# SyncE instead of GpSimd as the issuer of the transfers in a branch that is not taken: a graph-attention layer with layer norm

## The chip, the core and the metric

The kernel runs on one core of a Trainium2 chip. The time is device microseconds from launch to end, the median of several runs. A profile is one execution with a record of every instruction and every transfer; its span reaches from the first to the last instruction.

The engines are TensorE (PE; its weight loads are PEld), VectorE (DVE), ScalarE (ACT), GpSimd (POOL) and SyncE (SP), which computes nothing and here issues transfers. Each has an instruction queue of its own, run in order (in the views PEq or PEldq, DVEq, ACTq, POOLq, SPq are the parts that handle branches, semaphores and issues), and each waits for the others through counts (semaphores).

## The reference

One graph-attention layer with four heads, added to its input, then a layer norm of each row:

```python
# x (4096, 512), adj (4096, 4096), W (512, 4*512), a (4, 2*512, 1), all float32
ht = (x @ W).reshape(N, 4, 512).transpose(1, 0, 2)
src = einsum('hnd,hd->hn', ht, a[:, :512, 0])
dst = einsum('hnd,hd->hn', ht, a[:, 512:, 0])
e = leaky_relu(src[:, :, None] + dst[:, None, :], 0.01) + adj[None]
att = softmax(e, axis=-1)
out = layernorm(x + einsum('hij,hjd->hid', att, ht).mean(axis=0), axis=-1)
```

The non-zero entries of adj lie between 0.05 and 1e9, so in most rows the softmax is decided by the largest entry of adj alone. Then the row's attention is a one-hot vector, and the sum over nodes is a gather of one row of x.

## The kernel before

The kernel has two paths. `gat_resnorm_kernel` (L27) runs the usual path, `leading_rows` (L67), then reads a flag and runs `general` (L529) if the flag is over zero:

```python
    flag = nc.values_load(any_bad[0:1, 0:1], min_val=0, max_val=N)
    with tc.If(flag > 0, preferred_fallthrough_block=True, label="general"):
        general(tc, x, adj, W, out, ident, v, n_bad)
```

**The usual path** takes the 4096 rows in 32 blocks of 128 (partition p of block ib is row 32p + ib). A loop over t (L409) has its stages written out by hand: adj blocks are loaded five ahead on SyncE (L118), VectorE finds each row's largest entry by segments of 32 (L163 and L170 to L172), GpSimd gathers the segment (L176) and then the row of x that the largest entry names (L186) with indirect transfers, TensorE turns the gathered row (L213) and multiplies it by the mean of the four heads' W (L228), ScalarE and GpSimd make the statistics of the layer norm (L250 to L257) and ScalarE writes the result (L261). SyncE stores the finished rows at the end, in this order (L465 to L468 for the first ones, and then):

```python
    for ib, n in ((NB - 4, 1), (NB - 3, 1), (BEHIND, 2), (NB - 2, 1), (BEHIND + 2, 2)):
        store(nc.sync, ib, n)
    store(nc.sync, NB - 1, 1)
```

The last store is that of block 31, whose second half ScalarE writes at L310. All loads and stores of the usual path are in SyncE's queue except the two small ones of `a` (ScalarE, L128) and the gathers (GpSimd). The order is the order of the program text (`manual_schedule`, L51), on each queue.

**The flag.** A test on VectorE (L384 to L390) asks of each row whether its largest entry leads by enough that everything else vanishes; TensorE counts the rows (L394), and VectorE writes the number of the other rows to `any_bad` (L401). All five engines read it (L61) and branch (L62). In this profile the count is zero: no record stands on a line from 537 to 650, so none of the body is run.

**The general path**, the body of the conditional, computes the full attention. It loads x in eight pieces (L555) and W in four (L557), makes the scores' two halves, and then runs a loop over the 32 blocks; in a block with such rows, it loads adj (L592), computes the four heads, loads the block's x (L632), normalises, and stores the block (L643). Its waits, counts and the loop around it are put in by the framework (`tc.If`, `tc.For_i`). The framework rotates an issuer's transfers over a fixed set of counts; transfers from SyncE and from GpSimd use two different sets of eight (the two small loads on ScalarE use SyncE's set).

What follows L62 is the close of the program: SyncE waits until all counts have their final value, all engines meet in a barrier, GpSimd clears the counts, and a second barrier ends the program (all on L674 in the profile). On four engines, L410 marks where a hint for the branch at L62 is put (`HINTED`, L20: TensorE, ScalarE, VectorE and GpSimd, not SyncE); in the trace these hints stand at 0.9 to 1.1 us.

Of the kernel before, what the change touches and what calls it, by code (L numbers as in the profile page):

```python
# [20 lines left out]
P = 128  # L21
# [5 lines left out]
def gat_resnorm_kernel(  # L27
# [34 lines left out]
    with tc.If(flag > 0, preferred_fallthrough_block=True, label="general"):  # L62
        general(tc, x, adj, W, out, ident, v, n_bad)
# [464 lines left out]
@with_exitstack  # L528
def general(ctx, tc, x, adj, W, out, ident, v, n_bad):  # L529

    nc = tc.nc
    N, D = x.shape
    KB, NB, NCH, Q = D // P, N // P, N // C, C // P
    H = v.shape[2] // 2  # L540

    const = ctx.enter_context(tc.tile_pool(name="const", bufs=1))
    x_sb = const.tile([P, NB, D], F32, name="x_sb")
    dst_b = const.tile([P, H, N], F32, name="dst_b")
    src = const.tile([P, NB, H], F32, name="src")
    w_sb = const.tile([P, KB, H * D], F32, name="w_sb")
    x_blocks = x.rearrange("(nb p) d -> p nb d", p=P)
    w_blocks = W.rearrange("(kb p) m -> p kb m", p=P)

    with ExitStack() as pre:  # L550
        sd_all = pre.enter_context(tc.tile_pool(name="all", bufs=1)).tile([2 * H, N], F32, name="sd_all")
        two = pre.enter_context(tc.tile_pool(name="two", bufs=2))
        pps = pre.enter_context(tc.tile_pool(name="pps", bufs=2, space=bass.MemoryType.PSUM))
        for g in range(NCH):
            nc.gpsimd.dma_start(x_sb[:, ts(g, Q), :], x_blocks[:, ts(g, Q), :])  # L555
        for kb in range(KB):
            nc.gpsimd.dma_start(w_sb[:, kb, :], w_blocks[:, kb, :])  # L557
        for g in range(NCH):
            xT = two.tile([P, KB, C], F32, name="xT")
            for q in range(Q):  # L560
                ps = pps.tile([P, KB, P], F32, name="ps_x")
                for kb in range(KB):
                    nc.tensor.transpose(ps[:, kb, :], x_sb[:, g * Q + q, ts(kb, P)], ident)
                nc.scalar.copy(xT[:, :, ts(q, P)], ps)
            ps = pps.tile([2 * H, C], F32, name="ps_sd")
            for kb in range(KB):
                nc.tensor.matmul(ps, v[:, kb, :], xT[:, kb, :], start=(kb == 0), stop=(kb == KB - 1))
            sd = sd_all[:, ts(g, C)]
            nc.vector.tensor_copy(sd, ps)
            for h in range(H):  # L570
                pb = pps.tile([P, C], F32, name="ps_b")
                one_hot = ident[: 2 * H, H + h : H + h + 1].to_broadcast([2 * H, P])
                nc.tensor.matmul(pb, one_hot, sd, start=True, stop=True)
                nc.vector.tensor_copy(dst_b[:, h, ts(g, C)], pb)
        for g in range(NCH):
            pt = pps.tile([P, Q, 2 * H], F32, name="ps_s")
            for q in range(Q):
                rows_of = sd_all[:, ds(g * Q + q, P, NB)]
                nc.tensor.transpose(pt[:, q, :], rows_of, ident[: 2 * H, : 2 * H])
            nc.vector.tensor_copy(src[:, ts(g, Q), :], pt[:, :, :H])  # L580

    score = ctx.enter_context(tc.tile_pool(name="score", bufs=1))
    turned = ctx.enter_context(tc.tile_pool(name="turned", bufs=2))
    stat = ctx.enter_context(tc.tile_pool(name="stat", bufs=2))
    psum = ctx.enter_context(tc.tile_pool(name="psum_g", bufs=2, space=bass.MemoryType.PSUM))

    def block(ib):
        src_i = stat.tile([P, H], F32, name="src_i", bufs=1)
        nc.vector.tensor_copy(src_i, src[:, ds(ib, 1), :].rearrange("p o h -> p (o h)"))
        held = psum.tile([P, D], F32, name="o_ps", bufs=1)  # L590
        adj_t = score.tile([P, N], F32, name="adj_g")
        nc.gpsimd.dma_start(adj_t, adj[ds(ib, P, NB), :])  # L592
        for h in range(H):
            s = score.tile([P, N], F32, name="s")
            nc.scalar.activation(s, dst_b[:, h, :], AF.Identity, bias=src_i[:, h : h + 1])
            nc.vector.scalar_tensor_tensor(s, s, SLOPE, s, op0=OP.mult, op1=OP.max)
            m = stat.tile([P, 1], F32, name="m")
            nc.vector.tensor_tensor_reduce(
                out=s, in0=s, in1=adj_t, scale=1.0, scalar=LOWEST, op0=OP.add, op1=OP.max, accum_out=m
            )  # L600
            nc.vector.tensor_scalar_mul(m, m, -1.0)
            z = stat.tile([P, 1], F32, name="z")
            nc.scalar.activation(s, s, AF.Exp, bias=m, accum_out=z)
            y_ps = psum.tile([P, D], F32, name="y_ps")
            for c in range(NCH):
                ps = psum.tile([P, Q, P], F32, name="pt_ps")
                for q in range(Q):
                    nc.tensor.transpose(ps[:, q, :], s[:, ds(c * C + q * P, P)], ident)
                pt = turned.tile([P, Q, P], F32, name="pt")
                (nc.scalar.copy if c % 2 else nc.vector.tensor_copy)(pt, ps)  # L610
                for q in range(Q):
                    nc.tensor.matmul(
                        y_ps, pt[:, q, :], x_sb[:, c * Q + q, :],
                        start=(c == 0 and q == 0), stop=(c == NCH - 1 and q == Q - 1),
                    )

            nc.vector.tensor_scalar_mul(z, z, float(H))
            nc.vector.reciprocal(z, z)
            y = turned.tile([P, D], F32, name="y_g")
            nc.vector.tensor_scalar_mul(y, y_ps, z)  # L620
            ps = psum.tile([P, Q, P], F32, name="pt_ps")
            for q in range(Q):
                nc.tensor.transpose(ps[:, q, :], y[:, ts(q, P)], ident)
            yt = turned.tile([P, KB, P], F32, name="pt")
            nc.scalar.copy(yt, ps)
            for kb in range(KB):
                nc.tensor.matmul(
                    held, yt[:, kb, :], w_sb[:, kb, ts(h, D)],
                    start=(h == 0 and kb == 0), stop=(h == H - 1 and kb == KB - 1),
                )  # L630
        r = turned.tile([P, D], F32, name="y_g")
        nc.gpsimd.dma_start(r, x[ds(ib, P, NB), :])  # L632
        nc.vector.tensor_add(r, r, held)
        st = stat.tile([P, nc.vector.BN_STATS_DIM], F32, name="st_g")
        nc.vector.bn_stats(st, r)
        mv = stat.tile([P, nc.vector.BN_AGGR_DIM], F32, name="mv_g")
        nc.vector.bn_aggr(mv, st)
        sd = stat.tile([P, 1], F32, name="sd_g")
        nc.vector.tensor_scalar_add(sd, mv[:, 1:2], EPS)
        nc.scalar.activation(sd, sd, AF.Sqrt)  # L640
        nc.vector.reciprocal(sd, sd)
        nc.vector.tensor_scalar(r, r, mv[:, 0:1], sd, op0=OP.subtract, op1=OP.mult)
        nc.gpsimd.dma_start(out[ds(ib, P, NB), :], r)  # L643

    with tc.For_i(0, NB, 1) as ib:
        of_block = stat.tile([1, 1], I32, name="of_block", bufs=1)
        nc.vector.tensor_copy(of_block, n_bad[0:1, ds(ib, 1)])
        here = nc.values_load(of_block[0:1, 0:1], min_val=0, max_val=P)
        with tc.If(here > 0):
            block(ib)  # L650
# [28 lines left out]
```

## Time and profile before

| what | us |
|---|---|
| median of 3 runs (235.95 to 236.46) | 235.95 |
| the profiled execution's own time | 236.21 |
| its span, first to last instruction | 234.6 |
| TensorE busy | 195.2 (83%) |
| VectorE busy | 188.4 (80%) |
| ScalarE busy | 111.6 (48%) |
| GpSimd busy | 101.2 (43%) |
| last computing instruction (ScalarE, L310) | 230.7 to 231.3 |
| last store issued (SyncE, L313) | 231.3 |

The mean granted clock of TensorE is 0.975. A line of the view by group has line, engine, operation, destination and source, then count, shortest, median and longest duration in ns and the first and the last start. In the table by stage each engine has its busy us and its number of instructions in the stage, in the order PE, PEld, DVE, ACT, POOL; then come the granted clock, the DMA engines' busy share and GB/s. In the chain of waits a line has start, duration, engine, tile and line. In the list of DMA issues a line ends with the size of one transfer and the time from its issue to its landing. Instructions that branch, wait, issue or handle semaphores are not counted as busy.

### The profile page before, as it was taken

To read this page: it belongs to the slowest core of one execution; us is meant where nothing else is said; L and a number is where in the kernel's file an instruction comes from. 1 tells how busy PE (TensorE), PEld (TensorE's weight loads), DVE (VectorE), ACT (ScalarE), POOL (GpSimd) and SP (SyncE) were. 2 spreads that over 40 slices of the span, in tenths; PEclk is the share of its full clock that TensorE was granted. 3 is DMA by queue.
4 is the path that set the end of the run, shared out by engine and by line. 5 is a ranking of instruction groups with operands and counts; after the bars stand their busy time and mean duration, and the time that the engine had idled before them with its cause. 6 is when DMAs were issued, how large, how long until landed. Compare 5 with 4: busy or idle time off the path is not lost.

```text
span 234.6 us, 2498 instructions
## 1 busy us (share of the span) xinstructions
PE 195.2 (83%) x683; PEld 101.4 (43%) x683; DVE 188.4 (80%) x302; ACT 111.6 (48%) x267; POOL 101.2 (43%) x215
## 2 busy tenths in 40 slices
PE   0188929999999999999979879797998968698990
PEld 0034514756565655555534333242443423244460
DVE  1736875589869995999589989998799999989672
ACT  2012011255474747474758354646464645166582
POOL 1012232414527462646353645464365464549130
PEclk9999977999999999999999999999799999999998
DMA  6999999999999999999999999999999999999985
GB/s 226 439 428 426 443 425 430 415 440 412 440 420 426 424 437 434 425 424 428 427 432 433 425 433 422 432 418 429 425 432 418 422 425 427 411 425 419 417 355 210
DMA packets 13697, 97.21 MB, mean 414 GB/s; under 512 B 2152, under 2 KB 2664, under 8 KB 7792
## 3 DMA queue, kind: packets, MB, share of 16 engines
q1 hardware_dynamic: 10080, 88.08, 88.9%
q0 software_dynamic: 3584, 8.92, 9.6%
q8 instruction: 6, 0.10, 0.2%
q14 instruction: 11, 0.09, 0.1%
q10 hardware_dynamic: 16, 0.02, 0.0%
HBM read 88.62 MB, written 8.39 MB: 414 GB/s over the span
## 4 chain that ended last, share of the span: by engine, by line
DMA 45%; POOL 17%; issue 15%; PE 10%; DVE 9%; ACT 1%; POOLq 0%; SPq 0%; DVEq 0%
DMA adj_t<-in_adj_dram 42%; DVE seg L163 8%; PE o L228 7%; POOL lead L176 6%; POOL y L186 5%; DMA y<-in_x_dram,col 3%; POOL sd L256 2%; PE o L270 2%; POOL start L181 1%; POOL row L174 1%; POOL col L200 1%; PE tp L213 1%; PE o L221 1%; ACT yt L215 1%; POOL sd L255 1%
## 5 line engine op out<-in xcount | busy, mean ns | idle before, releaser
L163 DVE TENSOR_REDUCE seg<-adj_t 128x64 f32<-128x2048 f32 (+1 forms) x68 | 146.0, 2149 | 32.7 <-DMA adj_t<-in_adj_dram 32.3
L228 PE MATMUL o<-w_sum,yt 128*128 128x512 f32 x248 | 115.1, 605 | 1.7 <-ACT yt L215 1.7
L228 PEld LDWEIGHTS o<-w_sum,yt 128*128 128x128 f32 x248 | 44.5, 191 | 54.8 <-issue 42.3
L215 ACT COPY yt<-tp 128x512 f32<-128x512 f32 x32 | 18.8, 588 | 44.3 <-PE tp L213 44.3
L176 POOL DMA_INDIRECT lead<-in_adj_dram,row x32 | 32.3, 1010 | 15.5 <-POOL row L174 15.0
L186 POOL DMA_INDIRECT y<-in_x_dram,col x32 | 30.9, 965 | 15.4 <-POOL col L200 15.2
L318 PE MATMUL o<-hold,ident 128*128 128x512 f32 x32 | 18.9, 745 | 17.5 <-DMA hold<-in_L_gnn_W_dram 17.5
L213 PE MATMUL tp<-ident,y 128*128 128x128 f32 x128 | 20.0, 280 | 12.6 <-DMA y<-in_x_dram,col 12.6
L221 PE MATMUL o<-hold,ident 128*128 128x512 f32 x52 | 27.3, 611 | 0.0
L213 PEld LDWEIGHTS tp<-ident,y 128*128 128x128 f32 x128 | 14.9, 143 | 25.4 <-issue 25.0
L174 POOL TENSOR_TENSOR row<-at,first 128x1 uint32<-128x1 uint32 x32 | 6.1, 190 | 42.0 <-DVE at L172 42.0
L336 ACT COPY wt<-tp 128x512 f32<-128x512 f32 x16 | 9.2, 587 | 31.4 <-PE tp L334 31.4
L200 POOL TENSOR_TENSOR col<-start,within 128x1 uint32<-128x1 uint32 x31 | 5.9, 190 | 40.1 <-DVE within L198 40.1
L235 ACT ACTIVATE sq<-hold 128x512 f32<-128x512 f32 x32 | 19.8, 619 | 0.0
L342 PEld LDWEIGHTS pv<-at_d,wt 128*128 128x128 f32 x128 | 16.3, 191 | 6.8 <-ACT wt L336 4.0
L318 PEld LDWEIGHTS o<-hold,ident 128*128 128x128 f32 x32 | 7.4, 243 | 26.7 <-POOL row L174 11.0
L319 ACT ACTIVATE w_sum<-o 128x512 f32<-128x512 f32 x4 | 2.4, 598 | 33.9 <-PE o L318 33.9
L261 ACT ACTIVATE hold<-o,nm,sd 128x512 f32<-128x512 f32 x24 | 17.2, 771 | 0.0
L252 ACT ACTIVATE sq<-o,nm 128x512 f32<-128x512 f32 x24 | 16.5, 688 | 0.8
L342 PE MATMUL pv<-at_d,wt 128*128 128x2 f32 x128 | 15.3, 244 | 0.6 <-ACT wt L336 0.6
L250 ACT ACTIVATE sq<-o 128x512 f32<-128x512 f32 x24 | 14.6, 609 | 0.0
L334 PEld LDWEIGHTS tp<-ident,hold 128*128 128x128 f32 x64 | 7.9, 142 | 6.9 <-issue 6.9
(85 smaller groups left out, 139.8 us busy)
## 6 DMA issues: line engine op xcount, KB each, us to landing
adj_t<-in_adj_dram SPq DMA_DIRECT2D x27, 2048.0 KB, 31.3
hold<-in_x_dram SPq DMA_DIRECT2D x7, 1024.0 KB, 33.2
adj_t<-in_adj_dram SPq DMA_DIRECT2D x6, 1024.0 KB, 25.7
out_dram<-hold SPq DMA_DIRECT2D x10, 512.0 KB, 15.2
adj_t<-in_adj_dram SPq DMA_DIRECT2D x8, 512.0 KB
hold<-in_L_gnn_W_dram SPq DMA_DIRECT2D x4, 1024.0 KB
out_dram<-hold SPq DMA_DIRECT2D x2, 1024.0 KB
hold<-in_x_dram SPq DMA_DIRECT2D x2, 512.0 KB, 14.1
```

What stands on the lines that cost most here:

```text
L163: nc.vector.tensor_reduce(seg_of[ib][:, ts(k, S // n)], adj_t[ib][:, ts(k, N // n)].rearrange("p (s e) -> p s e", e=E), axis=AX.X, op=OP.max,)
L176: nc.gpsimd.indirect_dma_start(out=lead, out_offset=None, in_=adj_segs, in_offset=bass.IndirectOffsetOnAxis(ap=row[:, :1], axis=0),)
L186: nc.gpsimd.indirect_dma_start(out=y, out_offset=None, in_=x, in_offset=bass.IndirectOffsetOnAxis(ap=col[:, :1], axis=0),)
L213: nc.tensor.transpose(tp[:, kb, :], y[:, ts(kb, P)], ident)
L215: nc.scalar.copy(yt, tp)
L221: nc.tensor.matmul(o_ps[ib], ident, hold[:, ib, :], start=start, stop=False)
L228: nc.tensor.matmul(o_ps[ib], yt_of[ib][:, kb, :], w_sum[:, kb, :], start=(start and kb == 0), stop=(kb == KB - 1),)
L235: nc.scalar.activation(sq, hold[:, ib, :], AF.Square, accum_out=xx[:, ib : ib + 1])
L252: nc.scalar.activation(sq, o, AF.Square, bias=nm[:, i], accum_out=sd[:, i])
L261: nc.scalar.activation(hold[:, ib, :], o_ps.pop(ib), AF.Identity, bias=nm[:, i], scale=sd[:, i])
L318: nc.tensor.matmul(o, ident, hold[:, w_at + kb * H + h, :], start=(h == 0), stop=(h == H - 1))
L342: nc.tensor.matmul(pv[:, kb, h : 2 * H : H], wt[:, k, :], at_d[:, k, h : 2 * H : H], start=(k == 0), stop=(k == KB - 1),)
```

## The change

Five call sites in `general` issue their transfer from SyncE's queue in place of GpSimd's. Nothing in `leading_rows` changes, and `general` computes the same. In `general` no other instruction than these five, with what the framework puts around them, stands on SyncE or on GpSimd, apart from the loop and the test of L645 to L649, which all engines run.

```diff
         for g in range(NCH):
-            nc.gpsimd.dma_start(x_sb[:, ts(g, Q), :], x_blocks[:, ts(g, Q), :])
+            nc.sync.dma_start(x_sb[:, ts(g, Q), :], x_blocks[:, ts(g, Q), :])
         for kb in range(KB):
-            nc.gpsimd.dma_start(w_sb[:, kb, :], w_blocks[:, kb, :])
+            nc.sync.dma_start(w_sb[:, kb, :], w_blocks[:, kb, :])
...
         adj_t = score.tile([P, N], F32, name="adj_g")
-        nc.gpsimd.dma_start(adj_t, adj[ds(ib, P, NB), :])
+        nc.sync.dma_start(adj_t, adj[ds(ib, P, NB), :])
...
         r = turned.tile([P, D], F32, name="y_g")
-        nc.gpsimd.dma_start(r, x[ds(ib, P, NB), :])
+        nc.sync.dma_start(r, x[ds(ib, P, NB), :])
...
-        nc.gpsimd.dma_start(out[ds(ib, P, NB), :], r)
+        nc.sync.dma_start(out[ds(ib, P, NB), :], r)
```

With NCH = 8 and KB = 4 the first two sites are twelve transfers, issued once; the other three are issued once in each pass of the loop that has work.

## The prediction

> **What bounds the kernel now.** The first view is the page itself: its span, and the row of DMA shares over forty slices.
>
> ```profile
> span 234.6 us, 2498 instructions
> DMA  6999999999999999999999999999999999999985
> HBM read 88.62 MB, written 8.39 MB: 414 GB/s over the span
> ```
>
> The DMA engines are full from the second slice to the thirty-eighth. So the length of the body is that of 97 MB of transfers, and only the last two slices (the last 11.7 us) are open to anything else. The second view is the table by stage, and in it the stage after 231.3 us, ahead of which the chain of waits has its last computed piece.
>
> ```profile
> 231.30:234.60 3.30, 0.00 (x0) 0.00 (x0) 0.00 (x0) 0.00 (x0) 0.00 (x0) 0.77 0.26 98
> ```
>
> ```profile
> 230.69 0.56 ACT hold L310
> ```
>
> No engine computes in the last 3.3 us. ScalarE's L310 writes the last half row block, the last store leaves at 231.29, and then the program closes. The change touches only lines that are not run (the body of the conditional at L62), so the body of the kernel cannot feel it other than through what the conditional leaves on the path when it is not taken. That is what the third view, all instructions of L61 and L62, shows.
>
> ```profile
> L61 SPq TENSOR_LOAD <-any_bad x1: 517/517/517, 231.7 to 231.7; - x1
> L62 POOLq EVENT_SEMAPHORE  x5: 17/42/43, 226.3 to 226.6; - x5
> L62 PEldq EVENT_SEMAPHORE  x2: 51/51/51, 229.3 to 229.4; - x2
> L62 ACTq EVENT_SEMAPHORE  x2: 17/17/17, 231.9 to 232.0; - x2
> L62 DVEq EVENT_SEMAPHORE  x2: 21/21/21, 232.0 to 232.1; - x2
> L62 POOLq INC_SWDGE_SEM  x1: 1476/1476/1476, 226.7 to 226.7; - x1
> L62 SPq COMPARE_BRANCH  x1: 50/50/50, 232.6 to 232.6; - x1
> L62 SPq EVENT_SEMAPHORE  x1: 17/17/17, 232.7 to 232.7; - x1
> ```
>
> Each engine branches over the body, and then settles the counts that the body would have raised: TensorE, ScalarE and VectorE have two such instructions each (their compute count and their sequencer's), SyncE has one (its sequencer's), and GpSimd has one for its sequencer, four waits for seven transfer counts, and one instruction that waits for the eighth and raises all eight. In the single records, each settling instruction waits for its own count to have its value of the usual path and then adds to it. GpSimd has the transfers of the body, so it settles eight transfer counts, between 226.3 and 228.2 us, when nobody waits for it. SyncE has none and settles nothing but itself.
>
> The fourth view is the close, L674, on SyncE, in two windows: up to 233.5, and from there to 233.7.
>
> ```profile
> L674 SPq EVENT_SEMAPHORE  x11: 28/28/28, 232.8 to 233.5; - x11
> ```
>
> ```profile
> L674 SPq EVENT_SEMAPHORE  x1: 28/28/28, 233.6 to 233.6; - x1
> L674 SPq DRAIN  x1: 7/7/7, 233.7 to 233.7; - x1
> ```
>
> SyncE reads off 24 counts two at a time, in 12 instructions. Single records put the first at 232.834 and the eleventh at 233.458, so 0.062 us apart (0.624 / 10). The twelfth, which has the last store's count, starts at 233.619, 0.10 late: the records of semaphore updates put the sixteenth landing of that store at 233.603. Its issue and landing:
>
> ```profile
> out_dram<-hold SPq DMA_DIRECT2D x1, 256.0 KB, 2.3
> ```
>
> The drain follows at 233.687, and the barrier of all engines, which needs it, brings the end at 234.56. So two things end last together: the landing (233.603) and SyncE's own instructions, which without that landing would have drained at 232.834 + 12 x 0.062 = 233.58. SyncE has 0.10 us to spare, no more.
>
> **What the Trainium skill says.** The page Perfetto Trace Analysis, section Identifying Dependency Chains, says that waits that don't fit an instruction are put into EventSemaphore instructions ahead of it; the 12 of the close agree. The page DMA: Bandwidth & Descriptors, section on the anatomy of one DMA (told there for the GpSimd path), puts most of about 2 us of fixed cost in the receipt of the write; the last store's 2.3 us agrees and stays. The page Runtime: NRT & Kernel Launch, section Instruction fetch mechanics, says that a branch to a target outside the two blocks held has to wait for a fetch. In the trace SyncE's branch at 232.554 has its next instruction at 232.736, 0.18 us on, and ScalarE's hinted, longer jump takes 0.48 (231.411 to 231.894): no wait for a fetch is seen, but SyncE's jump gets longer.
>
> **The change part by part.**
>
> *Five call sites leave GpSimd's queue* (8 x and 4 W loads, and in the loop adj, x and out). On the usual path GpSimd loses its four waits and the 1.476 us raise at 226.7; its 5.3 us drain, which starts at 228.229, may shorten. All of that ends by 233.535, ahead of SyncE's drain at 233.687, and nothing computes on GpSimd after 225.5. Worth 0, and a gain is excluded, since the barrier waits for SyncE. What is late next would be SyncE in any case. The gathers of the usual path (L176, L186) stay on GpSimd, and no queue of transfers changes before L61.
>
> *Fifteen transfers, with their waits and addresses, enter SyncE's queue inside the body.* They are jumped over. Cost on the path 0 as instructions; as distance, some 40 more to jump (15 transfers, and by what GpSimd has there, about 25 waits and address operations). Bounds: 0 if the target is held, and about 1.9 us if not, the time from GpSimd's branch at 225.797 to the instruction fetch at 227.737 that follows it. I take 0: SyncE has run 110-odd instructions by then, its last fetch (8 KB) was at 188.6 us, and the target stays within the next block.
>
> *SyncE has to settle the transfer counts.* The 15 transfers rotate over eight counts, which the stores of the usual path raise as well: after 12 + 3 transfers each of the eight has been raised. So, after the pattern of the other engines, eight instructions that wait and add stand between SyncE's branch and its close. The price of one has two ends: 0.062 us, the close's interval of an instruction that only waits, and 0.098, from SyncE's own settling instruction (232.736) to the next one (232.834). I take 0.098. They would start at 232.834; the eighth could start at 232.834 + 7 x 0.098 = 233.52, but it waits for its own count to be complete, thus for the last store: 233.62. Queued behind it on SyncE is the whole close. Close starts at 233.62 + 0.098 = 233.72, the 12 instructions no longer wait for anything: drain at 233.72 + 12 x 0.062 = 234.46. Before it was at 233.687, so +0.78 us. At 0.062 each the eighth waits for the same landing: 233.62 + 0.062 + 0.744 = 234.43, +0.74. So what is paid is not the eight instructions, which lie beside the landing, but the close, which lay beside it and now comes after.
>
> *The close and the barrier*: same counts, same 12 instructions, other values to wait for. 0.
>
> The sum for the profiled execution: its own time is 236.21, of which 234.56 is the span and 1.65 lies around it; 236.21 + 0.78 = 236.99. It stands 0.26 above the median of the runs; on the median it is 235.95 + 0.78 = **236.73**, 0.33% more.
>
> **The rivals.**
>
> *B, order.* The last store's count is settled first, not last. Then the seven others follow the landing too: 233.62 + 8 x 0.062 to 0.098 + 0.744 = 234.86 to 235.15, +1.2 to +1.5: 237.1 to 237.4. For it: nothing fixes the order of the eight; against it: in the close the transfer counts of SyncE stand in their order of rotation, the last store's last.
>
> *C, raises without waits.* The instructions add and don't wait. Then the close meets the landing as now, only later: with 0.062 each the drain is at 233.33 + 0.744 = 234.07, +0.4; with fewer than eight it is less, from +0.1: 236.05 to 236.35. Against it: every settling instruction in the records has both.
>
> *D, not slower.* The settling isn't done on SyncE, but on an engine that has nothing left (ScalarE is through at 232.06, GpSimd at 228.2), or not at all: then the usual path on SyncE is as it was, and its 12 waits meet the landing at 233.6, at most 0.1 later for the passing on: 235.95 to 236.05. It decides if SyncE executes no more than one instruction (0.10 / 0.098) more after its branch. For it: the change leaves the usual path's code alone; against it: GpSimd's five settling waits and its raise stand on the engine that issues the transfers.
>
> *E, fetch.* The jump's target is not held: the fetch puts the first settling instruction 1.7 later (1.9 less the 0.18 that the jump takes anyway), and the eight and the close follow: 232.74 + 1.7 + 0.5 to 0.8 + 0.74 = 235.7 to 236.0, +2.0 to +2.3: 238.0 to 238.3. Against it: SyncE's fetch at 188.6 us.
>
> **How the numbers follow.** Chances: forecast 0.62, B 0.11, C 0.11, D 0.09, E 0.07. The range leaves out D, E and the bottom of C, some 0.19 together: 236.2 to 237.5; the forecast's own is 236.6 to 236.8. A measurement of this kernel can tell about 0.3% from no change, 0.7 us, so the line is at 236.66 and the forecast lies only just over it: of its 0.62 I put 0.37 above, with B and E 0.55 slower. Its other 0.25, C and nearly all of D make 0.43 for the same, and 0.02 is left for faster.
>
> **What would show it.** In the changed kernel's trace: L62 on SyncE with nine EVENT_SEMAPHORE in place of one, GpSimd with one and no INC_SWDGE_SEM; the last of the nine at 233.6 or just after the last landing; L674's 12 on SyncE all after that, 0.062 apart with no gap at the twelfth; everything before 231.3 us as it was. Nine instructions that end before the landing would show C; one, D; the last store's count waited for ahead of the others, B; over 1 us between SyncE's branch and its next instruction, E. If the stage up to 231.3 us changes by more than 0.3 us, the premise that the body is untouched is wrong.

## The result and the profile after

The changed kernel takes 237.01 us (median of 12 runs, 236.42 to 238.44), the kernel before 236.04 (12 runs). The ratio is 1.0038, 95% interval [1.0024, 1.0052]: 0.9 us more, 0.57 to 1.23. Forecast were +0.78 us and a range of 236.2 to 237.5. The profiled execution took 236.54 us with a span of 234.761; before it was 236.21 with 234.564.

The first view is the page after, its span, the DMA shares and the DMA queue that brings instructions.

```profile
span 234.8 us, 2501 instructions
DMA  6999999999999999999999999999999999999984
q14 instruction: 12, 0.10, 0.1%
```

The body is the same full row of DMA, and one packet more of instructions is fetched (12 in place of 11; where it stands is told below, with the jump). The span grew by 0.20 us only, and this is the sum of two opposite parts, which single records give. The last store was issued at 230.733 us, 0.553 earlier than before; from there to the end it takes 4.028 us in place of 3.278, 0.750 more. The second part is the effect of the change at the end. Of the first, 0.24 may come from the opening (the fourth view); the rest lies within the scatter of the body: in a second profile of the same changed kernel the last store is issued at 231.136 us, and over the fourteen profiles of this study between 230.6 and 232.3. So all that follows, the opening apart, is read from the issue of the last store on.

The second view is L62 in the kernel after.

```profile
L62 SPq EVENT_SEMAPHORE  x9: 17/17/17, 232.5 to 233.1; - x9
L62 POOLq EVENT_SEMAPHORE  x1: 17/17/17, 225.7 to 225.7; - x1
L62 SPq COMPARE_BRANCH  x1: 50/50/50, 232.0 to 232.0; - x1
```

SyncE has nine settling instructions in place of one, GpSimd has one in place of five, and the INC_SWDGE_SEM is gone. (The first of the nine is SyncE's own, as before; the eight others, for the transfer counts, are called raises below.) The third view is the close, L674 on SyncE, from 233.1 to 233.9 us: the twelve waits, and the drain, the record with which SyncE goes on from them to the barrier of all engines.

```profile
L674 SPq EVENT_SEMAPHORE  x12: 28/28/28, 233.2 to 233.8; - x12
L674 SPq DRAIN  x1: 7/7/7, 233.9 to 233.9; - x1
```

The twelve waits now start when the landing of the last store (232.996) is over; they run through without a gap, 0.061 us apart. Before, eleven of them lay ahead of it. In single records, as us after the issue of the last store:

```
                                      before   after
last store landed                      2.317   2.263
SyncE branches (L62)                   1.268   1.262
from the branch to its next record     0.182   0.495
first wait of the close                1.548   2.422
drain of SyncE                         2.401   3.163
end of the span                        3.278   4.028
```

The drain comes 0.762 later. SyncE starts its close 0.874 later (2.422 - 1.548), and gets back 0.112 since the close no longer waits for the landing (0.741 long in place of 0.853).

The fourth view is the opening, L665: GpSimd's rows before, then SyncE's after.

```profile
L665 POOLq MOVE  x4: 29/29/35, 0.2 to 0.4; - x4
L665 POOLq EVENT_SEMAPHORE  x2: 17/17/17, 0.8 to 0.9; - x2
```

```profile
L665 SPq MOVE  x4: 29/34/42, 0.0 to 0.2; - x4
L665 SPq EVENT_SEMAPHORE  x1: 17/17/17, 0.7 to 0.7; - x1
```

This was not forecast. Four register moves have gone from GpSimd, which opens the first barrier, to SyncE, which has time ahead of it. The barrier opens earlier, and the first load is issued at 0.740 us in place of 0.977. (The start of the span is not what moved: VectorE's first record stands at 0.12 us before and at 0.13 after, ScalarE's at 0.14 and 0.15.)

### The profile page after: what moved, and what is told of

It reads as the page before. It is cut to its first block, busy times and chain, and to the rows that moved or that the text cites. A ratio compares the mean times of both kernels' runs of the same rounds, so it can differ in the third digit from the quotient of the medians.

```text
span 234.8 us, 2501 instructions
## 1 busy us (share of the span) xinstructions
PE 196.8 (84%) x683; PEld 101.9 (43%) x683; DVE 187.8 (80%) x302; ACT 111.6 (48%) x267; POOL 100.8 (43%) x215
## 4 chain that ended last, share of the span: by engine, by line
DMA 45%; POOL 18%; issue 16%; DVE 9%; PE 8%; ACT 1%; POOLq 0%; SPq 0%; DVEq 0%
DMA adj_t<-in_adj_dram 42%; DVE seg L163 8%; POOL lead L176 6%; POOL y L186 5%; PE o L228 5%; DMA y<-in_x_dram,col 3%; POOL sd L256 2%; PE o L270 2%; POOL start L181 1%; POOL row L174 1%; POOL col L200 1%; PE tp L213 1%; ACT yt L215 1%; POOL sd L255 1%; DVE at L172 0%
## 5 line engine op out<-in xcount | busy, mean ns | idle before, releaser
L318 PE MATMUL o<-hold,ident 128*128 128x512 f32 x32 | 20.4, 796 | 14.7 <-DMA hold<-in_L_gnn_W_dram 14.7
L221 PE MATMUL o<-hold,ident 128*128 128x512 f32 x52 | 27.3, 611 | 0.0
```

Source lines behind the costliest of these rows:

```text
L221: nc.tensor.matmul(o_ps[ib], ident, hold[:, ib, :], start=start, stop=False)
L318: nc.tensor.matmul(o, ident, hold[:, w_at + kb * H + h, :], start=(h == 0), stop=(h == H - 1))
```

## The experiments

The theory is that of the prediction: SyncE settles eight transfer counts, and the close, which lay beside the last store's landing, comes after. The rivals: the longer jump is what costs; or the time comes from the body or the place of the code. All edits are in `general`, which is not run, or ahead of it. This table has what each showed, in us after the issue of the last store, with the time against runs of the kernel before on the same chip:

```
                     counts   branch    first     landed  drain   ratio, 95% interval
                     settled  to next   wait of
                     on SP    record    close
before                  0      0.18      1.55      2.32    2.40
after                   8      0.50      2.42      2.26    3.16   1.0038 [1.0024, 1.0052]
after once more         8      0.50      2.42      2.25    3.16   1.0031 [1.0019, 1.0044]
eight x loads           8      0.18      2.38      2.29    3.12   1.0032 [1.0010, 1.0054]
seven x loads           7      0.18      2.05      2.30    2.80   1.0006 [0.9991, 1.0022]
one (adj)               1      0.18      1.63      2.29    2.37   1.0002 [0.9982, 1.0022]
15 on ScalarE           8      0.18      2.43      2.34    3.17   1.0042 [1.0025, 1.0058]
jump, 15 loads          0      0.50      1.85      2.30    2.60   1.0020 [1.0008, 1.0032]
jump, 10 loads          0      0.50      1.86      2.29    2.61   1.0005 [0.9992, 1.0017]
jump, 60 loads          0      2.60      3.96      2.28    4.71   1.0093 [1.0060, 1.0127]
after, 8 x on GpSimd    8      0.50      2.43      2.34    3.17   1.0079 [1.0037, 1.0120]
after, no x loads       7      0.50      2.35      2.27    3.09   1.0041 [1.0012, 1.0070]
three of the loop       3      0.50      2.08      2.40    2.82   1.0031 [1.0008, 1.0053]
the same, hinted        3      0.53      2.11      2.26    2.85   1.0044 [1.0027, 1.0061]
```

### Eight counts, short jump

```diff
-            nc.gpsimd.dma_start(x_sb[:, ts(g, Q), :], x_blocks[:, ts(g, Q), :])
+            nc.sync.dma_start(x_sb[:, ts(g, Q), :], x_blocks[:, ts(g, Q), :])
```

> Only the eight x loads are issued by SyncE; the body stays short on SyncE. Measure: from the issue of the last store to SyncE's drain at the close, 2.40 us before, 3.16 us after the change. Theory of the prediction (eight settling instructions, the eighth held by the last store's landing, the close behind it): eight raises on SyncE, the last at about 0.02 us after the landing, drain 0.80 us after the landing, so 3.13 to 3.18, and the time 0.7 to 0.8 us above before. Rival (the longer jump is what costs): the jump is short again, 0.18 us, and the time goes back by about 0.3 us, to 2.85.

Measured: a jump of 0.18 us, the eighth raise 0.02 us after the landing and 0.33 after the seventh, the drain at 3.12. L62 and the close in this kernel (the last store was issued at 231.484 and landed at 233.775):

```profile
L62 SPq EVENT_SEMAPHORE  x9: 17/17/17, 232.9 to 233.8; - x9
L674 SPq EVENT_SEMAPHORE  x12: 28/28/28, 233.9 to 234.5; - x12
```

So the eight counts alone, without the longer jump, bring nearly the whole difference (0.72 of 0.76 us), and the rival's 2.85 falls.

### Seven counts, the last store's not among them

```diff
-            nc.gpsimd.dma_start(x_sb[:, ts(g, Q), :], x_blocks[:, ts(g, Q), :])
+            (nc.sync if g < NCH - 1 else nc.gpsimd).dma_start(x_sb[:, ts(g, Q), :], x_blocks[:, ts(g, Q), :])
```

> As with the eight x loads, but only seven of them on SyncE: the last store's own count has not to be settled, and nothing among the seven waits for the landing. Theory of the landing (the eighth instruction waits for the store and holds the close): seven raises end about 2.05 us after the issue of the last store, the close runs beside the landing, and the twelfth wait finds it done: drain at 2.78 us, in place of 3.12 to 3.17 with eight. Rival (each raise costs its own time and the landing plays no part): 3.12 less one raise, 3.05. Time 0.4 us above before by the first, 0.65 by the second.

Measured: drain at 2.80, 0.33 less than with eight, for one instruction that takes 0.07. L62 and, with its first and last start, the close in this kernel (the last store was issued at 231.445):

```profile
L62 SPq EVENT_SEMAPHORE  x8: 17/17/17, 232.9 to 233.4; - x8
L62 POOLq INC_SWDGE_SEM  x1: 1476/1476/1476, 226.8 to 226.8; - x1
L674 SPq EVENT_SEMAPHORE  x12: 27/28/28, 233.5 to 234.2; - x12
```

SyncE passes from the settling to the close at 233.495, 0.25 ahead of the landing (233.745), and the close lies in part beside it again. What the eighth costs in these two kernels is the wait for the last store, and not itself. GpSimd settles eight counts here as well, early, and at no cost that shows at SyncE's drain. The time is no more than 0.5 us above that of before and can't be told from it.

### One count

```diff
-        nc.gpsimd.dma_start(adj_t, adj[ds(ib, P, NB), :])
+        nc.sync.dma_start(adj_t, adj[ds(ib, P, NB), :])
```

> Only the adj load of the loop on SyncE: one count to settle, and not that of the last store. Theory (SyncE has 0.10 us to spare before the landing ends): one raise of about 0.09 us fits into it, drain at 2.40 to 2.43 us from the issue of the last store, and the time as before. Rival (each settled count costs its whole instruction, in the close too): 2.5.

Measured: drain at 2.37, 0.085 us after the landing, as before (0.084). One raise fits into the 0.10 us that SyncE had to spare; the time is the same within its interval.

### The transfers on ScalarE

```diff
-            nc.gpsimd.dma_start(x_sb[:, ts(g, Q), :], x_blocks[:, ts(g, Q), :])
+            nc.scalar.dma_start(x_sb[:, ts(g, Q), :], x_blocks[:, ts(g, Q), :])
...
-        nc.gpsimd.dma_start(out[ds(ib, P, NB), :], r)
+        nc.scalar.dma_start(out[ds(ib, P, NB), :], r)
```

(and so at the three sites between)

> All 15 transfers of the body are issued by ScalarE, so the settling is done there, by an engine that is through before SyncE. Theory of the prediction: SyncE has its single settling instruction again, ScalarE the eight, its last one at the landing; SyncE's close has it about 0.1 us later: 2.4 to 2.5 us, time 0 to 0.1 above before. Rival (the time comes from another source than SyncE's end, as the body of the kernel or the place of the code): as slow as after the change, +0.8 to +1.0.

Measured: as slow as the change, and not for the rival's reason. L62 shows it:

```profile
L62 SPq EVENT_SEMAPHORE  x9: 17/17/17, 232.0 to 233.0; - x9
L62 ACTq EVENT_SEMAPHORE  x2: 17/17/17, 231.3 to 231.4; - x2
```

The eight instructions stand on SyncE again, though ScalarE issues every transfer of the body. So the expectation of both theories rested on a wrong premise: the framework settles these eight counts on SyncE also when ScalarE issues. The end has the same course as with eight x loads (drain at 3.17; the eighth raise starts 0.389 us after the seventh and 0.016 after the landing). The kernel couldn't tell what it was built for, since the settling did not move; it shows that the end is the same with ScalarE as issuer as with SyncE.

### The jump alone

```diff
+    for _ in range(15):
+        nc.values_load(n_bad[0:1, 0:1], engines=[mybir.EngineType.SP], min_val=0, max_val=P)
     with ExitStack() as pre:
```

> The kernel before, with 15 register loads on SyncE added in the body of the conditional, which is not taken; all transfers of the body stay on GpSimd. SyncE jumps over as many instructions as after the change, and has no transfer count to settle. Theory of the prediction (the jump is free): 2.40 us from the last store to the drain, time as before. Rival (the jump costs what the profile after shows, 0.50 us in place of 0.18): +0.31 less the 0.10 to spare, so 2.6, and the time 0.2 us above before.

Measured: 0.50 us to the next record and a drain at 2.60, about 2.40 + 0.31 - 0.10; the time is 1.0020 [1.0008, 1.0032], 0.2 to 0.8 us. The jump is not free: here the theory of the prediction falls. With 10 loads in place of 15:

> The jump alone again, with 10 register loads in place of 15: SyncE jumps to the 194th of its instructions in place of the 209th[...]. If the cost is that of leaving the stretch, the branch is back at 0.18 us to the next instruction and the drain at 2.40 us. If it grows with distance: about 0.45 and 2.55. Time as before, or 0.15 above.

Measured: again 0.50 and 2.61, and neither branch of the expectation held. Counted in the built programs, SyncE jumps to its 164th instruction before, to its 173rd to 177th in the kernels with 0.18 us, and to its 191st to 209th in those with 0.50: a step somewhere between the 177th and the 191st, not a slope over these distances. That the step is the border of a stretch, the piece of the program that one fetch brings, fits; but I had placed that border between the 194th and the 209th, which was wrong. The instruction queue says more. In all eight profiles with 0.50 or 0.53 us an 8 KB packet of instructions starts 1.05 to 1.08 us after SyncE's branch; in the five with 0.18 none does. This is what that queue moves after the change from 232.9 us on (the branch is at 231.995), and what moves at all with the eight x loads from 233.5 on (the branch is at 232.738):

```profile
q14 instruction: 1, 0.01, 2.1%
```

```profile
DMA packets 0, 0.00 MB, mean 0 GB/s; under 512 B 0, under 2 KB 0, under 8 KB 0
```

So the longer jump goes together with a fetch of further instructions, as it would at a border. SyncE does not wait for that packet, since its next record stands 0.5 us ahead of it; what takes the 0.32 us is not shown. With 60 loads (the target is the 344th):

> The jump alone, with 60 register loads: the target is the 344th instruction of SyncE[...]. Theory of rival E in the prediction: the branch waits for a fetch, 1.6 to 2.0 us to the next instruction, drain at 3.8 to 4.2 us after the issue of the last store, time 1.4 to 1.8 above before. If the target is fetched ahead: 0.5 and 2.6, time 0.2 above.

```profile
L62 SPq COMPARE_BRANCH  x1: 45/45/45, 232.9 to 232.9; - x1
L62 SPq EVENT_SEMAPHORE  x1: 17/17/17, 235.5 to 235.5; - x1
```

Between the two lies 2.60 us in which SyncE has nothing to wait for but its instructions; an 8 KB instruction packet starts 0.94 us after the branch, and here the next record comes after it. That is rival E of the prediction, at a higher price than the 1.9 us it had, and above the 1.6 to 2.0 expected here; the drain is at 4.71, and the ratio is 1.0093. The Trainium skill's page Runtime: NRT & Kernel Launch, section Instruction fetch mechanics, says that such a branch waits for a fetch; this run agrees, with packets of 8 KB where the page has blocks of 16.

### The changed kernel once more

> The changed kernel once more, for a second profile. Both theories: 3.1 to 3.2 us from the last store to the drain, nine settling instructions on SyncE, time 0.7 to 1.0 above before. If its runs scatter more than those of before again (236.4 to 238.4 against 235.6 to 236.5) the scatter belongs to the kernel; the profile shows whether it stands in the body or in the end.

Measured: drain at 3.16, a ratio of 1.0031, runs from 236.49 to 237.63. The end repeats to 0.01 us, while the last store is issued 0.40 us later than in the first profile: the scatter is that of the body, and not the changed kernel's own, since the kernel before had 235.62 to 238.53 beside it.

### The part outside the span

The runs list time and span of every execution. Their difference was 1.57 us before (median of 58) and 1.83 after (17): 0.26 us that no view of the span explains. Two kernels were to find out what it goes with. The first puts the eight x loads on GpSimd as well, in front of those on SyncE:

```diff
+            nc.gpsimd.dma_start(x_sb[:, ts(g, Q), :], x_blocks[:, ts(g, Q), :])
             nc.sync.dma_start(x_sb[:, ts(g, Q), :], x_blocks[:, ts(g, Q), :])
```

> The changed kernel, with its eight x loads issued once more from GpSimd in the body that is not run: SyncE settles its eight counts, and GpSimd settles eight as before. Asked is the part of the time that lies outside the span, 1.57 us before (median of 58 runs) and 1.83 after the change. If it goes with GpSimd's settling: back to 1.57. If it goes with SyncE's eighth count: 1.83. The start is as after the change (first load issued 0.24 us earlier than before, since four address moves leave GpSimd), and from the last store to the drain 3.16 us in either case. Time 0.5 us above before by the first, 0.75 by the second.

The second leaves SyncE seven transfers and GpSimd none:

```diff
-        for g in range(NCH):
-            nc.sync.dma_start(x_sb[:, ts(g, Q), :], x_blocks[:, ts(g, Q), :])
+        nc.vector.memset(x_sb, 0.0)
```

> The other half: in the body that is not run, the eight x loads are left out (a fill with zeros stands in their place), so SyncE settles seven counts, not that of the last store, and GpSimd none. If the part outside the span goes with GpSimd's settling: 1.83 us; if with SyncE's eighth count: 1.57. The jump is the long one (0.50 us), the seven raises have no landing to wait for: drain 3.1 us after the issue of the last store. Time 0.7 us above before by the first, 0.45 by the second.

Measured: 1.80 us outside in the first (5 runs) and 1.88 in the second (6 runs), so neither GpSimd's settling nor the eighth count is the reason; both suspicions fall. Drains at 3.17 and 3.09, ratios 1.0079 [1.0037, 1.0120] and 1.0041 [1.0012, 1.0070]. The second ratio agrees with the expectation; the first, 0.9 to 2.8 us, is above the 0.5 to 0.75 expected, and since its end is that of the changed kernel, the rest lies in the body of its five runs and is not explained. The third kernel moves only the three transfers of the loop, the fourth adds a hint:

```diff
-HINTED = tuple(getattr(mybir.EngineType, name) for name in ("PE", "Activation", "DVE", "Pool"))
+HINTED = tuple(getattr(mybir.EngineType, name) for name in ("PE", "Activation", "DVE", "Pool", "SP"))
```

> Only the three transfers of the loop, whose addresses are computed, are issued by SyncE; the twelve others stay on GpSimd. The start should be as after the change, 0.24 us earlier; the part outside the span 1.57 us. Three counts to settle, none with the landing: with a jump of 0.50 us (as in the run with ten register loads, whose target is the same) the close starts 2.10 us after the issue of the last store and the drain is at 2.85; with 0.18 it is at 2.54. Time 0.2 us above before by the first, 0.1 below by the second.

> The same, and SyncE is added to the four engines that get a hint for the branch. If the hint shortens SyncE's jump, 0.18 us to the next instruction and the drain 2.54 us after the last store, time 0.1 us below before. If it doesn't (ScalarE's hinted jump takes 0.48 us in every profile): 0.50 and 2.85, time 0.2 above.

Measured: jumps of 0.50 and 0.53 us, drains at 2.82 and 2.85, outside 1.80 and 1.84, ratios 1.0031 [1.0008, 1.0053] and 1.0044 [1.0027, 1.0061]. The hint does not shorten SyncE's jump. The part outside was expected at 1.57 and isn't, and the hinted kernel's time (0.6 to 1.4 us above before, in four runs) is above the 0.2 expected. Over all kernels one thing goes with the larger part outside: the early opening. Where the first load is issued at 0.73 to 0.86 us (after, the 15 on ScalarE, and these last four) it is 1.80 to 1.90; where at 0.97 to 0.99, it is 1.56 to 1.62, with one exception, the eight x loads (1.71). So what the span gains at the opening seems to be missing from the time. It is seen together and not shown as a cause, and why is open.

## Why the prediction held, and where its terms were off

*SyncE has 0.10 us to spare.* Right: one raise is free (2.37), a jump that is 0.32 longer costs 0.20.

*Eight settling instructions on SyncE.* Right in number and place. The reason given against rival D, that the settling stands on the engine that issues, was wrong: with ScalarE as issuer it stands on SyncE too. D is out for another reason than the one I gave. B is out since the last store's count is settled as the last of the eight, and C since the eighth raise waits (0.33 us with the eight x loads).

*0.098 us each.* Too high: the eight take 0.571 together (232.584 to 233.155), 0.071 each. Where the landing holds the eighth this makes no difference. In the changed kernel nothing holds it, and eight at 0.098 would have ended 0.21 us later.

*The jump at 0.* Wrong: 0.50 us in place of 0.18. Alone it costs 0.20. That no fetch is waited for was right.

*The eighth held by the landing, the close behind it.* In the changed kernel itself the landing (232.996) is just over when the eighth starts (233.088), since the jump put the raises 0.31 later. So this is not what ends last there: jump and raises together reach 2.42, where the landing alone would have let the close start at 2.38 (the eight x loads). The changed kernel without its x loads says the same: it keeps the long jump and settles seven counts, not the last store's, and its drain comes at 3.09, only one raise ahead of 3.16. That a raise held by the landing pushes the close behind it is shown by the pair of seven and eight counts with the short jump (2.80 and 3.12), and it would have set almost the same end.

*The close, 12 x 0.062.* Right: 0.741.

*The sum.* +0.78 forecast, +0.76 measured at the drain in both profiles of the changed kernel (0.762 and 0.756). The terms that set it differ: 0.313 for the jump, 0.57 for the raises, less 0.11 that the close no longer waits. That a free jump, a higher price and a wait gave the same total is luck: the two ways end within 0.05 us of each other (2.42 and 2.38). What holds in both is that eight raises on SyncE put the whole close behind the landing.

*Everything before 231.3 us as it was.* Wrong by 0.24 us at the opening: the prediction looked at what GpSimd loses at the end and left out that the register moves for the loop's addresses stand at the opening. By its own sign, a change of more than 0.3 us in the stage up to 231.3, the premise would have fallen, since the last store left 0.55 earlier; but two profiles of the changed kernel differ by 0.40 there, so the sign was finer than the scatter. The 0.24 us didn't spoil the sum since the part outside the span grew by 0.26, which is luck again: -0.24 + 0.75 + 0.26 = +0.77, against measured +0.90 (0.57 to 1.23) and +0.73 (0.45 to 1.04) in the second set.

No kernel of the study beats the one before. The nearest are the short jump with one or seven counts and the jump over ten loads, whose close lies in part beside the landing; their times can't be told from that of before.

## What to carry to other kernels

A body that is not run still leaves something on the path: each count that it would raise is settled after the branch, and the engine that settles it may not be the one that issues. Look at who ends last at the close, and what that engine has to spare; work that is free on an engine that is through early (here GpSimd, which begins to settle 8 us before the end) costs time on the last one as soon as what that one has to spare (here 0.10 us) is used up. A settling instruction that waits for a transfer still in flight brings everything queued behind it after that transfer, so one count more can cost several times its own instruction (0.33 us for 0.07).

## What the runs showed of the hardware

- A taken branch on SyncE has three prices: 0.18 us to its next instruction with the target near, 0.50 with the target 27 to 45 instructions further, 2.60 with it 180 further. With the second, and not with the first, an instruction packet follows 1.05 to 1.08 us after the branch. The second takes as long as the hinted jump of ScalarE (0.48), and a hint leaves it at 0.53.
- An instruction on SyncE that waits for a count that is there and adds to it takes 0.07 us from one to the next when several stand in a row, 0.08 to 0.10 for the first ones; one that only waits for two counts takes 0.061.
- Register moves of the opening, on the engine that opens the first barrier, delay the first load: four on GpSimd, 0.24 us in the span. In the time of an execution the gain of moving them to SyncE did not show.
